# A two-layer graph network on one core: the first chunks of the query and key weights, the value weights and the last weight each in a slot of their own, and the last batch's softmax sums by folds with its norms in another order

## The chip, the cores and the metric

The kernel runs on one core of a Trainium2 chip. The metric is the device time of one execution in microseconds, as the median of several runs. All times below are microseconds (us) of that device time or of the span of one profiled execution.

## The reference

Two layers over a batch of 32 graphs with the same 512 nodes and the same adjacency matrix; each node has 512 features. Everything is float32.

```
x: (32, 512, 512), adj: (512, 512) of zeros and ones, symmetric, ones on its diagonal

def layernorm(x): (x - mean) / sqrt(var + 1e-5)        # over the last axis, no weights

# layer 0: attention over neighbours, 8 heads of 64
q, k, v = x @ Wq + bq, x @ Wk + bk, x @ Wv + bv        # (32, 512, 512), seen as 8 heads of 64
scores  = q k^T / sqrt(64) + (-1e9 where adj == 0)     # (32, 8, 512, 512)
x = layernorm(x + softmax(scores) @ v)

# layer 1: graph convolution
x = layernorm(x + ((adj @ x) @ W1 + b1))
```

## The kernel before

**Units of matmul work.** TensorE (PE) works in 128 by 128 tiles with 512 columns. The products with weights are split products: each float32 operand is split into a high part and a rest of fp32r type, and a product takes three passes, HIGH, REST and BOTH (a combination of the two), of four 128x512 matmuls each. One such unit of 12 matmuls makes 128 columns of q or k (`project`, L396 by way of `one_pass`), 128 rows of v (`project_values`), or 128 rows of the convolution (`convolve`). The parts of an operand are made by three instructions: ACT makes the high part (`split_high` L298, for weights `split_weight` L308), DVE the rest (L301, L309), and POOL or DVE the combination (L304, L312, L318).

**A batch.** For each batch: 8 units for q and k, 4 for v, the scores of four pairs of heads (`scores` L565, 16 matmuls of 64x512 per pair, two pairs at a time in `take_scores`), the mask added by DVE (L567, 16 operations for two pairs) and the exponential by ACT (L569), the sums of the exponentials over the four key blocks by POOL (L580), and the product with v (`attend` L588). Then the aggregation adj times x (`aggregate` L509, for the last batch `aggregate_rows` L530), whose halves are made by `split` (L483, L485) or `split_rows` (L518, L519), and the convolution with its residual (L542, L543). Layer norms are `statistics` (L455, L456), `square_root` (L459 on ACT), `invert_root` (L464, L465 on DVE) and `normalise` (L470 on ACT).

**Order.** The order of all instructions is written by hand: under `manual_schedule` each engine, and SP which issues nearly all DMAs, takes its instructions in the order in which the program calls them, and waits for the data of each. `first_half(b)` runs the product with v for two pairs, the 8 projection units of batch b+1 with other work behind each (the lists in `behind`, merged in by `merge`), and the scores of the other two pairs. `second_half(b)` runs the rest of b's attention, the v units of b+1, b-1's aggregation and convolution, and the first scores of b+1. The last batch has an order of its own, `last_halves`, and a tail in the kernel's main part. `ahead`, `seen` and `next_` there are lists of normalisations and statistics that are put between the units of the last convolutions.

**Slots.** Tiles are named by tags, and a tag has a fixed number of slots. A new tile waits until all readers of the tile that lay in its slot are done. The tags that matter here: `wv` and `w1` (one slot each: the split value weights and the split last weight W1), `xs` (two: adjacency at the start, then batches of x and the raw W1), `stream` (three: chunks of the split q and k weights), `e` (8: raw weights at the start, then exponentials) and `turn` (6: blocks of x).

**Chunks of the query and key weights.** The weights of q and k are split once, in 8 chunks (n = 0 to 7: q0, k0, q1, k1 and so on) by `make_chunk` (ACT and DVE) and `finish_chunk` (DVE), while batch 0 is projected with them. Each is written to DRAM by `keep_chunk` (L383), and from batch 1 on fetched back for each batch by `fetch_chunk` (L391), three ahead; `project` fetches chunk n+3 when it has used chunk n. In the kernel before, chunks 0 to 3 are made in the slot of `wv` and chunks 4 to 7 in that of `w1`:

```
        if n % DB == 0:
            EARLY[n // DB] = work.tile([P, DB, 3, DB, P], FR, name="early", tag=("wv", "w1")[n // DB], bufs=1)
```

So the value weights are split (`split_values_weight`) when chunks 0 to 3 have been written out, and W1 is split (`split_last_weight`) late, at the end of `second_half(0)`; its raw form is loaded before the attention of batch 0.

**Sums of the softmax.** For the sums over the keys, POOL's result still has to be added over 128 partitions and brought to the layout of the rows. In all batches but the last, `fold_squares` does it on DVE: it transposes in squares of 32 (L619) and reduces (L622, twice per pair), and after two pairs writes the parts to DRAM (L627); `fetch_parts` reads them back in four DMAs (L634) and `add_up` adds and inverts (L640, L641). The outputs of these batches come back to rows by way of DRAM too (`turn_out` L602 and L604, `fetch_rows` L610) and are scaled by ACT (L654). The last batch has its sums from PE: `sum_queries` (L670) multiplies by a column of ones, 32 matmuls of one column per two pairs, and `invert_sums` (L676, L677) inverts them. Its outputs are transposed by PE (`turn_back` L685) and scaled and added by DVE (`last_residual` L689, L691).

**Other names.** `stay_warm` issues matmuls on zeros at the start, `load_squares` loads a block of x of a later batch in four DMAs (L232), `look_for_low_half` tests adj, and `judge` makes a verdict on the data, which the 1x1 matmul in the last loop gathers; another kernel for general inputs runs behind it, and does not run for these data.

Of the kernel before, what the change touches and what calls it, by code (L numbers as in the profile page):

```python
# [18 lines left out]
P = 128  # L19
# [163 lines left out]
def fast_kernel(ctx: ExitStack, tc, verdict, x, adj, Wq, bq, Wk, bk, Wv, bv, W1, b1, out):  # L183
# [34 lines left out]

    def load_block(b, c):
        IN[b, c] = work.tile([P, D], FP, name="xin", tag="turn", bufs=TURNS)  # L220
        nc.sync.dma_start(IN[b, c], x[b, c * P:(c + 1) * P, :])

    def load_squares(b, d):

# [135 lines left out]
    SEQUENCE = [(which, m) for m in range(DB) for which in "qk"]  # L360
    CHUNK, KEPT = {}, {}
    AHEAD = 3
    EARLY, MADE = {}, {}

    def chunk():
        return work.tile([P, 3, DB, P], FR, name="stream", bufs=AHEAD)
# [1 line left out]
    def make_chunk(n):  # L368

        which, m = SEQUENCE[n]  # L370
        if n % DB == 0:
            EARLY[n // DB] = work.tile([P, DB, 3, DB, P], FR, name="early", tag=("wv", "w1")[n // DB], bufs=1)
        made = MADE[n] = CHUNK[0, which, m] = EARLY[n // DB][:, n % DB, :, :, :]
        split_weight(made[:, HIGH, :, :], made[:, REST, :, :], RAW[which, m // 2][:, m % 2, :, :])

    def finish_chunk(n):
# [235 lines left out]
    def fold_squares(b, hp):  # L612

        if hp % PAIRS == 0:
            PART[b, hp // PAIRS] = work.tile([P, P // SQ, NB, GROUP], FP, name="part", bufs=1)
        part = PART[b, hp // PAIRS]
        es = ES.pop((b, hp))
        square = SQUARES.pop((b, hp))
        nc.vector.transpose(square.rearrange("p s n -> p (s n)"), es.rearrange("p s n -> p (s n)"))  # L619
        squares = [square[:, s, :] for s in range(2)]  # L620
        for s in range(2):
            nc.vector.tensor_reduce(part[:, :, :, 2 * (hp % PAIRS) + s].rearrange("p i c -> p c i"),  # L622
                                    squares[s].rearrange("p (c i f) -> p c i f", c=NB, f=SQ), axis=AX.X,
                                    op=ALU.add)
        if hp % PAIRS == PAIRS - 1:
            PASSED[b, hp // PAIRS] = passing.tile([P, P // SQ, NB * GROUP], FP, name="passed")
            nc.sync.dma_start(PASSED[b, hp // PAIRS], part.rearrange("p i c h -> p i (c h)"))  # L627
# [29 lines left out]
        cols = X[b][:, :, hp * P:(hp + 1) * P]  # L657
        nc.gpsimd.tensor_add(cols, cols, ROWS.pop((b, hp)))

    SUMS = {}  # L660

    def sum_queries(b, g):

        sums = SUMS[b, g] = bank(NB, GROUP)
        for hp in range(g * PAIRS, (g + 1) * PAIRS):
            es = ES.pop((b, hp))
            for s in range(2):
                for c in range(NB):
                    h = 2 * (hp % PAIRS) + s
                    nc.tensor.matmul(sums[:, c, h:h + 1], es[:, s, c * P:(c + 1) * P], ones[:, 0:1],  # L670
                                     start=True, stop=True)

    def invert_sums(b, g):
        both = work.tile([P, 2, NB, GROUP], FP, name="inverse")
        total, inverse = both[:, 0, :, :], both[:, 1, :, :]
        nc.vector.tensor_copy(total, SUMS.pop((b, g)))  # L676
        nc.vector.reciprocal(inverse, total)  # L677
        nc.gpsimd.tensor_add(watched, watched, both)
        INVERSE[b, g] = inverse

    def turn_back(b, hp):

        pt = OUT[b, hp] = bank(NB, 2, HD)
# [27 lines left out]
    def stay_warm(times):  # L711
        for _ in range(times):
            nc.tensor.matmul(pm, still, still, start=True, stop=True)

    stay_warm(7)
    x_transpose(0)
    x_both(0, nc.gpsimd)
    make_chunk(0)
    stay_warm(4)
    for c in range(1, NB):  # L720
        x_transpose(c)
        x_both(c, nc.gpsimd if c < NB - 1 else nc.vector)
# [2 lines left out]
    make_chunk(1)  # L725
    finish_chunk(0)
    finish_chunk(1)
    for n in range(2):
        keep_chunk(n)

    def split_values_weight(d):
        w = RAW["v", d // 2][:, d % 2, :]
# [1 line left out]
        both_of_weight_beside(wv[:, BOTH, d, :], wv[:, REST, d, :], w)  # L734

    def split_last_weight(d):
        split_weight(w1[:, HIGH, d, :], w1[:, REST, d, :], w1_raw[:, d, :])
        both_of_weight(w1[:, BOTH, d, :], w1[:, HIGH, d, :], w1[:, REST, d, :])

    def norm(t, which):  # L740
# [31 lines left out]
    def first_half(b):  # L772

        attend(b, 0)
        turn_out(b, 0)
        attend(b, 1)
        turn_out(b, 1)
        fold_squares(b, 0)
        seen, old = survey(b - 2)[NB // 2:], norm(b - 1, 1)
        fresh, young = survey(b - 1, 0), norm(b - 1, 0)  # L780
        scaled, added = residuals(b, 0)
        squares = [(load_squares, b + 2, d) for d in range(DB // 2)]
        if b == 0:
            seen = [(look_for_low_half, c) for c in range(NB)]
        behind = [[(fetch_rows, b, 0)] + seen, [(fetch_rows, b, 1), (fold_squares, b, 1)] + old[:1], old[1:4],
                  [(fetch_parts, b, 0)] + old[4:],
                  [(take_scores, b, 1)] + ([(store, b - 2)] if b > 1 else []),
                  [(add_up, b, 0)] + fresh[:2], fresh[2:] + [(load, b)] + scaled[:1], young[:2] + scaled[1:],
                  added + young[2:] + squares]
        units = projections(b + 1)  # L790
        run(merge(units[:4] + [(list,)] + units[4:], behind))

    def second_half(b):

        splits, gathered = aggregation(b - 1)
        scaled, added = residuals(b, 1)
        turned, divided = turns(b + 2), splits_of_x(b + 2)
        squares = [(load_squares, b + 2, d) for d in range(DB // 2, DB)]
        early_seen = survey(b - 1) if b < B - 2 else []
        attend(b, 2)  # L800
        turn_out(b, 2)
        run(squares[:1])
        fold_squares(b, 2)
        attend(b, 3)
        fetch_rows(b, 2)
        turn_out(b, 3)
        fold_squares(b, 3)
        run(squares[1:])
        fetch_rows(b, 3)
        fetch_parts(b, 1)  # L810
        units = values(b + 1)
        if b == 0:
            run(units[:2] + [(take_scores, 1, 0)] + units[2:] + turned + divided + [(add_up, 0, 1)] + scaled + added)
            run([(split_last_weight, d) for d in range(DB)])
            return
        run(merge(units, [splits[:1], splits[1:2], splits[2:3], splits[3:] + turned[:1]]) + biases(b - 1))
        run(merge(gathered, [turned[1:2], turned[2:3], turned[3:] + [(add_up, b, 1)]]))
        if b == B - 2:
            load(B - 1)
        take_scores(b + 1, 0)  # L820
        run(merge(convolution(b - 1)[:NB if b < B - 2 else NB // 2],
                  [scaled[:1], early_seen[:1], early_seen[1:2]]))
        run(divided + scaled[1:] + added)

    def last_halves(b):

        splits, gathered = aggregation(b - 1)
        attend(b, 0)
        turn_out(b, 0)
        attend(b, 1)  # L830
        turn_out(b, 1)
        sum_queries(b, 0)
        take_scores(b, 1)
        turn_back(b, 0)
        turn_back(b, 1)
        run(survey(b - 1, 0) + norm(b - 1, 0))
        run(convolution(b - 2)[NB // 2:] + [(invert_sums, b, 0)] + splits)
        attend(b, 2)
        turn_out(b, 2)
        attend(b, 3)  # L840
        turn_out(b, 3)
        run([(last_residual, b, 0), (last_residual, b, 1)])
        turn_back(b, 2)
        turn_back(b, 3)
        sum_queries(b, 1)
        run(gathered[:2] + [(invert_sums, b, 1), (last_residual, b, 2), (last_residual, b, 3)] + gathered[2:])

    units = projections(0)
    ends = project_first_two()
# [2 lines left out]
        finish_chunk(n)  # L852
    run(ends)
    adjacency(0)
    for n in range(2, 4):
        keep_chunk(n)
    for d in range(2):
        load_squares(1, d)
    wv = None
    for n in range(2, len(units)):  # L860
        if n + 2 < len(units):
            make_chunk(n + 2)
# [1 line left out]
        run(units[n:n + 1])  # L864
        if n < 5:
            adjacency(n - 1)
        elif n == 5:
            wv = work.tile([P, 3, DB, N], FR, name="wv", bufs=1)
        if n > 4:
            split_values_weight(n - 5)  # L870
    split_values_weight(DB - 1)
    for n in range(4, len(units)):
        keep_chunk(n)
    for n in range(AHEAD):
        fetch_chunk(len(SEQUENCE) + n)
    for d in range(2, DB):
        load_squares(1, d)
    w1 = work.tile([P, 3, DB, N], FR, name="w1", bufs=1)
    w1_raw = work.tile([P, DB, D], FP, name="xs", bufs=2)
    nc.sync.dma_start(w1_raw, W1.rearrange("(c p) f -> p c f", p=P))  # L880
    b1_r = load_row(nc, consts, b1, "b1_r")
    take_scores(0, 0)
    run(merge(values(0), [[unit] for unit in turns(1)]))
# [8 lines left out]
    rest, final = convolution(t - 1), convolution(t)  # L892
    ahead, seen, next_ = norm(t, 0), survey(t - 1), norm(t, 1)
    run(biases(t - 1) + survey(t, 0) + ahead[:2])
    run(rest[:1])
    for c in range(NB):
        run(ahead[2 + c:3 + c])
        split_rows(t, c)
        run(rest[1 + c:2 + c])
    for c in range(NB):  # L900
        add_bias(t, c)
    run(survey(t - 2) + norm(t - 1, 1))
    store(t - 2)
    run(seen + next_[:2])
    aggregate_rows(t)
    well = judge()
    for table, name, shape in ((STAT, "stat", (2 * NB, 2)), (RSTD, "rstd", (2 * NB,)), (SHIFT, "shift", (2 * NB,))):
        table[t + 1] = work.tile([P, *shape], FP, name=name, bufs=3)
    for r, unit in enumerate(final):
# [9 lines left out]
        else:  # L919
            normalise(t + 1, NB + r)  # L920
        store(t, [r])
        if r == 0:
            run(next_[2:])
            store(t - 1)
        if r == 1:
            pm = bank(N)
            nc.tensor.matmul(pm[0:1, 0:1], well, ones[:, 0:1], start=True, stop=True)
# [25 lines left out]
```

## Time and profile before

| | us |
|---|---|
| three runs | 2655.01, 2658.06, 2660.86 |
| their median | 2658.06 |
| the profiled execution | 2655.91 |
| its span | 2654.1 |
| PE busy | 2621.1 (99%) |
| DVE busy | 2178.0 (82%) |
| POOL busy | 1765.3 (67%) |
| ACT busy | 1592.3 (60%) |

The mean granted TensorE clock of the profiled execution is 0.993 of full speed. Shares of busy time are shares of the span. In the views that follow, an engine's idle time is listed before the instruction that it waited for, with an arrow to what released it; where several semaphores were waited for, the one named is that which came last by the profile. "PEld" is TensorE's weight load, "SPq" the queue of SP, which issues DMAs.

### The profile page before, as it was taken

The page shows a single profiled execution, that of the slowest core. Times are in us where ns is not written, and L with a number is a line of the kernel's source. Part 1 is how long each engine was busy: PE and PEld are TensorE (multiplying, and loading weights), DVE is VectorE, ACT ScalarE, POOL GpSimd, SP SyncE. Part 2 cuts the span into 40 slices and gives each one's busy share as a digit, 9 for nine tenths or more (in the row PEclk, how much of TensorE's full clock was granted, in tenths as well). Part 3 has the DMA queues.
Part 4 walks back from the last instruction along what each step waited for, and adds up shares of the span by engine and source line. Part 5 has one row for each costly group of instructions (what it writes and reads, how often), then busy time and mean ns, then how long its engine had stood idle before and what let it go on. Part 6 is the DMA issues. An engine that isn't in the chain of part 4 may idle for free.

```text
span 2654.1 us, 35600 instructions
## 1 busy us (share of the span) xinstructions
PE 2621.1 (99%) x11394; PEld 1717.2 (65%) x11394; DVE 2178.0 (82%) x3513; ACT 1592.3 (60%) x2618; POOL 1765.3 (67%) x1087
## 2 busy tenths in 40 slices
PE   9989999999999999999999999999999999999997
PEld 6556666666666666666666666666666666666665
DVE  7868888888888888888888888888888888888867
ACT  4457556566556575565665565765665755656653
POOL 4556677676686666776766766666766667667663
PEclk9989999999999999999999999999999999999999
DMA  8565445664446654456644456544466544565411
GB/s 250 161 161 152 110 119 150 177 170 136 115 119 169 177 159 113 120 139 177 174 148 111 116 159 177 160 125 116 130 177 176 149 110 121 152 177 163 122 33 49
DMA packets 672832, 379.28 MB, mean 143 GB/s; under 512 B 585344, under 2 KB 589440, under 8 KB 672640
## 3 DMA queue, kind: packets, MB, share of 16 engines
q1 hardware_dynamic: 672640, 376.95, 51.8%
q8 instruction: 92, 1.51, 0.2%
q14 instruction: 100, 0.82, 0.1%
HBM read 302.45 MB, written 74.38 MB: 142 GB/s over the span
## 4 chain that ended last, share of the span: by engine, by line
PE 94%; DMA 2%; DVE 2%; ACT 1%; SPq 1%; issue 0%; DVEq 0%; ACTq 0%
PE bank L396 50%; PE bank L565 18%; PE bank L588 17%; PE bank L509 9%; DMA stream<-kept_k 2%; DVE factors L301 0%; DVE bnst L455 0%; DMA xin<-in_x_dram 0%; PE bank L670 0%; SPq L240 0%; ACT rows L654 0%; SPq L232 0%; DMA xs<-in_adj_dram 0%; DVE w L309 0%; DVE wv L309 0%
## 5 line engine op out<-in xcount | busy, mean ns | idle before, releaser
L396 PE MATMUL bank<-factors,stream 128*128 128x512 f32 x2976 | 703.1, 395 | 12.7 <-DMA stream<-kept_k 10.3
L396 PEld LDWEIGHTS bank<-factors,stream 128*128 128x128 f32 x2976 | 555.5, 189 | 182.5 <-issue 41.8
L580 POOL TENSOR_TENSOR es<-e 128x1024 f32<-128x1024 f32 x128 | 306.8, 2397 | 527.6 <-ACT e L569 527.6
L567 DVE SCALAR_TENSOR_TENSOR e<-gap,bank 128x512 f32<-128x512 uint8 x1024 | 617.3, 678 | 15.0 <-PE bank L565 14.8
L580 POOL TENSOR_TENSOR es<-es,e 128x1024 f32<-128x1024 f32 x256 | 614.2, 2399 | 20.1
L569 ACT ACTIVATE e<-e 128x1024 f32<-128x1024 f32 x512 | 509.8, 1050 | 47.7 <-DVE e L567 31.6
L304 POOL TENSOR_TENSOR factors<-factors,factors 128x512 fp32r<-128x512 f32 x253 | 359.1, 1434 | 213.0 <-DVE factors L301 212.1
L565 PE MATMUL bank<-q,k 64*128 64x512 f32 x2048 | 480.7, 604 | 2.6 <-ACT q L407 1.9
L588 PE MATMUL bank<-e,v 128*64 128x512 f32 x2048 | 453.6, 595 | 0.0
L565 PEld LDWEIGHTS bank<-q,k 64*128 64x128 f32 x2048 | 219.6, 187 | 233.6 <-issue 153.8
L396 PE MATMUL bank<-w,factors 128*128 128x512 f32 x1536 | 361.7, 394 | 4.2 <-ACT factors L298 3.3
L654 ACT ACTIVATE rows<-rows,zero,inverse 128x64 f32<-128x64 f32 x992 | 341.0, 426 | 31.1 <-POOL es L580 22.2
L298 ACT ACTIVATE factors<-bank 128x512 fp32r<-128x512 f32 x132 | 78.5, 597 | 468.4 <-PE bank L509 464.0
L396 PE MATMUL bank<-wv,factors 128*128 128x512 f32 x1536 | 357.8, 392 | 0.0
L396 PEld LDWEIGHTS bank<-w,factors 128*128 128x128 f32 x1536 | 286.3, 188 | 88.7 <-ACT e L569 22.7
L396 PEld LDWEIGHTS bank<-wv,factors 128*128 128x128 f32 x1536 | 285.7, 188 | 84.8 <-ACT xs L470 24.3
L588 PEld LDWEIGHTS bank<-e,v 128*64 128x64 f32 x2048 | 141.4, 137 | 278.4 <-issue 276.3
L509 PE MATMUL bank<-adjT,halves 128*128 128x512 f32 x960 | 229.6, 396 | 0.0
L470 ACT ACTIVATE xs<-xs,shift,rstd 128x512 f32<-128x512 f32 x248 | 184.1, 803 | 48.7 <-DVE shift L465 48.7
L509 PEld LDWEIGHTS bank<-adjT,halves 128*128 128x128 f32 x960 | 180.8, 188 | 43.6
L407 ACT ACTIVATE q<-bank,bq_c 128x512 f32<-128x512 f32 x128 | 86.9, 679 | 194.9 <-PE bank L396 194.9
L487 POOL TENSOR_TENSOR halves<-xs,halves 128x512 fp32r<-128x512 f32 x120 | 151.8, 1298 | 62.3 <-ACT halves L483 62.3
(96 smaller groups left out, 2522.1 us busy)
## 6 DMA issues: line engine op xcount, KB each, us to landing
stream<-kept_q SPq DMA_DIRECT2D x124, 768.0 KB, 6.1
stream<-kept_k SPq DMA_DIRECT2D x124, 768.0 KB, 5.0
xin<-in_x_dram SPq DMA_DIRECT2D x496, 64.0 KB, 2.8
turned<-attT SPq DMA_DIRECT2D x124, 256.0 KB, 2.3
rows<-turned SPq DMA_DIRECT2D x496, 64.0 KB, 3.6
xs<-in_x_dram SPq DMA_DIRECT2D x31, 1024.0 KB, 7.1
out_dram<-xs SPq DMA_DIRECT2D x31, 1024.0 KB, 5.5
part<-passed SPq DMA_DIRECT2D x248, 8.0 KB, 3.6
```

The lines of the kernel that those rows point to most:

```text
L304: engine.tensor_sub(both, plain(high), plain(rest))
L396: nc.tensor.matmul(pm, left(f, d), right(f, d), start=(f != REST and d == 0), stop=(f != HIGH and d == DB - 1))
L407: nc.scalar.activation(t, near, AF.Identity, bias=bias[:, m:m + 1], scale=1.0 + EPSILON)
L470: nc.scalar.activation(row, row, AF.Identity, bias=SHIFT[t][:, slot:slot + 1], scale=RSTD[t][:, slot:slot + 1])
L487: nc.gpsimd.tensor_sub(low, cols, plain(high))
L509: nc.tensor.matmul(pm, part, adjT[:, n % NB, :], start=(n == 0), stop=(n == 2 * NB - 1))
L565: nc.tensor.matmul(ps[s], keys[:, j * P:(j + 1) * P], queries, start=True, stop=True)
L567: nc.vector.scalar_tensor_tensor(e[:, s, :], gap[:, j, :], NEG * root, ps[s], op0=ALU.mult, op1=ALU.add)
L569: nc.scalar.activation(e, e, AF.Exp, scale=1.0 / root)
L580: nc.gpsimd.tensor_add(ES[b, hp], ES[b, hp] if j > 1 else E[b, hp, 0], E[b, hp, j])
L588: nc.tensor.matmul(po[s * HD:(s + 1) * HD, :], V[b, j][:, h * HD:(h + 1) * HD], e[:, s, :], start=(j == 0), stop=(j == NB - 1))
L654: nc.scalar.activation(part, part, AF.Identity, bias=zero, scale=inverse[:, c, s:s + 1])
```

## The change

- Of batch 0's four blocks of x, the second and fourth are loaded from ACT's queue; two of the matmuls of `stay_warm` go.
- Chunks 0 to 3 lie in one tile in the slot of `w1`, chunks 4 to 6 in the three slots of `stream`, and chunk 7 in one slot of `xs`. `wv` has its slot from the start. `split_values_weight` stands behind units 4 to 7 instead of 5 to 7 and their end. The writes of all chunks stand after the units, chunks 0 to 2, then half the squares of x of batch 1, chunks 3 to 7, the other squares, and the first three fetches.
- W1 is loaded in `first_half(0)`, behind the third unit, and split behind the first unit of `first_half(1)`.
- The last batch has its sums by `fold_squares`, `fetch_parts` and `add_up` like the others; `sum_queries` and `invert_sums` go. The order of the statistics, norms and biases of the last three batches changes, and `store` of the last but one batch stands before the last convolution.

```
     def load_block(b, c):
-        nc.sync.dma_start(IN[b, c], x[b, c * P:(c + 1) * P, :])
+        (nc.scalar if c % 2 else nc.sync).dma_start(IN[b, c], x[b, c * P:(c + 1) * P, :])
...
     def make_chunk(n):
-        if n % DB == 0:
-            EARLY[n // DB] = work.tile([P, DB, 3, DB, P], FR, name="early", tag=("wv", "w1")[n // DB], bufs=1)
-        made = MADE[n] = CHUNK[0, which, m] = EARLY[n // DB][:, n % DB, :, :, :]
+        if n < DB:
+            made = early[:, n, :, :, :]
+        elif n < DB + AHEAD:
+            made = chunk()
+        else:
+            made = work.tile([P, 3, DB, P], FR, name="last_chunk", tag="xs", bufs=2)
+        MADE[n] = CHUNK[0, which, m] = made
...
     def fold_squares(b, hp):
-        square = SQUARES.pop((b, hp))
-        nc.vector.transpose(square.rearrange("p s n -> p (s n)"), es.rearrange("p s n -> p (s n)"))
-        squares = [square[:, s, :] for s in range(2)]
+        if b == B - 1:
+            squares = [work.tile([P, N], FP, name="square", tag="turn", bufs=TURNS) for _ in range(2)]
+            for s in range(2):
+                nc.vector.transpose(squares[s], es[:, s, :])
+        else:
...
-    def sum_queries(b, g):
...
-    def invert_sums(b, g):
...
+    early = work.tile([P, DB, 3, DB, P], FR, name="early", tag="w1", bufs=1)
     stay_warm(7)
...
-    stay_warm(4)
+    stay_warm(2)
...
-    for n in range(2):
-        keep_chunk(n)
+    def load_last_weight():
+        RAW["w1"] = work.tile([P, DB, D], FP, name="xs", bufs=2)
+        nc.sync.dma_start(RAW["w1"], W1.rearrange("(c p) f -> p c f", p=P))
...
     def first_half(b):
         if b == 0:
-            seen = [(look_for_low_half, c) for c in range(NB)]
+            seen, old = [(look_for_low_half, c) for c in range(NB)], [(list,), (load_last_weight,)]
+        if b == 1:
+            seen = [(split_last_weight, d) for d in range(DB)]
...
     def second_half(b):
         if b == 0:
             run(units[:2] + [(take_scores, 1, 0)] + units[2:] + turned + divided + [(add_up, 0, 1)] + scaled + added)
-            run([(split_last_weight, d) for d in range(DB)])
             return
...
     def last_halves(b):
         attend(b, 0)
         turn_out(b, 0)
+        fold_squares(b, 0)
         attend(b, 1)
         turn_out(b, 1)
-        sum_queries(b, 0)
         take_scores(b, 1)
         turn_back(b, 0)
         turn_back(b, 1)
-        run(survey(b - 1, 0) + norm(b - 1, 0))
-        run(convolution(b - 2)[NB // 2:] + [(invert_sums, b, 0)] + splits)
+        fold_squares(b, 1)
+        fetch_parts(b, 0)
+        run(survey(b - 1, 0) + norm(b - 1, 0) + convolution(b - 2)[NB // 2:] + splits)
         attend(b, 2)
         turn_out(b, 2)
         attend(b, 3)
         turn_out(b, 3)
-        run([(last_residual, b, 0), (last_residual, b, 1)])
         turn_back(b, 2)
         turn_back(b, 3)
-        sum_queries(b, 1)
-        run(gathered[:2] + [(invert_sums, b, 1), (last_residual, b, 2), (last_residual, b, 3)] + gathered[2:])
+        run([(add_up, b, 0)] + folds(b, 1) + [(fetch_parts, b, 1), (last_residual, b, 0), (last_residual, b, 1)])
+        run(merge(gathered, [[unit] for unit in survey(b - 2)]) + norm(b - 1, 1))
+        store(b - 2)
+        run([(add_up, b, 1), (last_residual, b, 2), (last_residual, b, 3)])
...
-    for n in range(2, 4):
-        keep_chunk(n)
-    for d in range(2):
-        load_squares(1, d)
-    wv = None
+    wv = work.tile([P, 3, DB, N], FR, name="wv", bufs=1)
     for n in range(2, len(units)):
...
-        elif n == 5:
-            wv = work.tile([P, 3, DB, N], FR, name="wv", bufs=1)
-        if n > 4:
-            split_values_weight(n - 5)
-    split_values_weight(DB - 1)
-    for n in range(4, len(units)):
+        if n > 3:
+            split_values_weight(n - 4)
+    for n in range(AHEAD):
         keep_chunk(n)
+    for d in range(2):
+        load_squares(1, d)
+    for n in range(AHEAD, len(units)):
+        keep_chunk(n)
+    for d in range(2, DB):
+        load_squares(1, d)
     for n in range(AHEAD):
         fetch_chunk(len(SEQUENCE) + n)
-    for d in range(2, DB):
-        load_squares(1, d)
     w1 = work.tile([P, 3, DB, N], FR, name="w1", bufs=1)
-    w1_raw = work.tile([P, DB, D], FP, name="xs", bufs=2)
-    nc.sync.dma_start(w1_raw, W1.rearrange("(c p) f -> p c f", p=P))
...
     run(biases(t - 1) + survey(t, 0) + ahead[:2])
-    run(rest[:1])
     for c in range(NB):
         run(ahead[2 + c:3 + c])
         split_rows(t, c)
-        run(rest[1 + c:2 + c])
+        run(rest[c:c + 1] + seen[c:c + 1])
     for c in range(NB):
         add_bias(t, c)
-    run(survey(t - 2) + norm(t - 1, 1))
-    store(t - 2)
-    run(seen + next_[:2])
+    run(next_[:2])
     aggregate_rows(t)
+    run(next_[2:])
+    store(t - 1)
     well = judge()
...
-        if r == 0:
-            run(next_[2:])
-            store(t - 1)
```

More of the change, by code (lines that the diff above doesn't have):

```diff
@@ L362, in fast_kernel @@
     AHEAD = 3
-    EARLY, MADE = {}, {}
+    MADE = {}
     def chunk():
@@ L617, in fold_squares @@
         es = ES.pop((b, hp))
-        square = SQUARES.pop((b, hp))
-        nc.vector.transpose(square.rearrange("p s n -> p (s n)"), es.rearrange("p s n -> p (s n)"))
-        squares = [square[:, s, :] for s in range(2)]
+        if b == B - 1:
[3 more added lines that the diff above has]
+        else:
+            square = SQUARES.pop((b, hp))
+            nc.vector.transpose(square.rearrange("p s n -> p (s n)"), es.rearrange("p s n -> p (s n)"))
+            squares = [square[:, s, :] for s in range(2)]
         for s in range(2):
@@ L658, in add_rows @@
         nc.gpsimd.tensor_add(cols, cols, ROWS.pop((b, hp)))
-    SUMS = {}
-    def sum_queries(b, g):
[L664 to L671, printed above, removed]
-    def invert_sums(b, g):
[L674 to L679, printed above, removed]
     def turn_back(b, hp):
@@ L736, in split_last_weight @@
     def split_last_weight(d):
-        split_weight(w1[:, HIGH, d, :], w1[:, REST, d, :], w1_raw[:, d, :])
+        split_weight(w1[:, HIGH, d, :], w1[:, REST, d, :], RAW["w1"][:, d, :])
         both_of_weight(w1[:, BOTH, d, :], w1[:, HIGH, d, :], w1[:, REST, d, :])
```

## The prediction

> **What bounds the kernel now.** I read the page first: its busy times and the chain that ended last.
>
> ```profile
> PE 2621.1 (99%) x11394; PEld 1717.2 (65%) x11394; DVE 2178.0 (82%) x3513; ACT 1592.3 (60%) x2618; POOL 1765.3 (67%) x1087
> PE 94%; DMA 2%; DVE 2%; ACT 1%; SPq 1%; issue 0%; DVEq 0%; ACTq 0%
> ```
>
> TensorE (PE) works 2621.1 of 2654.1 us; only the 33 us in which it doesn't can be won without taking matmuls away. The view by windows says where they lie (columns: window, length, busy time of PE, its weight loads, DVE, ACT, POOL, then granted clock, DMA share, GB/s):
>
> ```profile
> 20.00:40.00 20.00, 16.57 (x66) 11.36 (x65) 13.31 (x22) 9.07 (x17) 1.63 (x2) 0.95 0.94 294
> 130.00:160.00 30.00, 19.27 (x57) 12.65 (x57) 19.09 (x27) 10.02 (x24) 8.00 (x7) 0.72 0.45 117
> 200.00:300.00 100.00, 100.00 (x437) 66.07 (x436) 84.92 (x140) 63.49 (x104) 70.24 (x43) 1.00 0.43 117
> 2560.00:2580.00 20.00, 20.00 (x96) 11.11 (x93) 7.31 (x13) 8.98 (x15) 11.54 (x7) 0.83 0.00 0
> 2620.00:2640.00 20.00, 16.64 (x62) 11.74 (x61) 17.80 (x44) 7.35 (x14) 5.54 (x4) 0.91 0.14 52
> 2640.00:2655.00 15.00, 4.53 (x20) 3.38 (x19) 6.53 (x18) 4.46 (x8) 0.00 (x0) 0.81 0.39 144
> ```
>
> Idle PE: 3.4 us in 20:40, 10.7 in 130:160, 3.4 and 10.5 at the end, none in 200:300. The order of the instructions of the two programs agrees on every engine, waits included, from the middle of the second batch to the last; so whatever is won at 40 or 160 us is carried to the end by a PE that is never idle, and only three stretches need a sum. I read each in the timeline (start, duration, engine, line; idle time before and its releaser in brackets):
>
> ```profile
> 29.79 0.63 ACT L283 ACTIVATE adjT<-attT 128x512 fp32r<-128x512 f32 x1 [2.13 <-DVE attT L282]
> 36.11 0.63 ACT L308 ACTIVATE wv<-e 128x512 fp32r<-128x512 f32 x1 [4.59 <-DMA xin<-in_x_dram]
> 42.00 9.64 DVE L567 SCALAR_TENSOR_TENSOR e<-gap,bank 128x512 f32<-128x512 uint8 x16
> ...
> 139.37 1.35 DVE L309 SCALAR_TENSOR_TENSOR w<-xs,w 128x512 fp32r<-128x512 f32 x1 [6.05 <-ACT w L308]
> 147.12 0.41 SPq L391 DMA_DIRECT2D stream<-kept_k  x1
> 152.06 5.46 PE L396 MATMUL bank<-factors,stream 128*128 128x512 f32 x12 [8.38 <-DMA stream<-kept_k]
> 158.67 9.65 DVE L567 SCALAR_TENSOR_TENSOR e<-gap,bank 128x512 f32<-128x512 uint8 x16 [0.35 <-PE bank L565]
> ...
> 2565.18 4.98 PE L670 MATMUL bank<-ones,es 128*128 128x1 f32 x32
> 2570.09 9.33 PE L565 MATMUL bank<-q,k 64*128 64x512 f32 x32
> 2572.26 1.28 DVE L567 SCALAR_TENSOR_TENSOR e<-gap,bank 128x512 f32<-128x512 uint8 x2 [13.30 <-PE bank L565]
> 2594.12 3.63 PE L670 MATMUL bank<-ones,es 128*128 128x1 f32 x32
> 2629.55 0.30 ACT L459 ACTIVATE rstd<-stat,eps 128x4 f32<-128x4 f32 x1 [0.27 <-DVE stat L456]
> 2642.27 0.17 DVE L464 RECIPROCAL rstd<-rstd 128x1 f32<-128x1 f32 x1 [1.54 <-ACT rstd L459]
> ```
>
> At 36.11 ACT waits 4.59 us for wv's slot. Chunks 0 to 3 lie there, and the last of their writes to DRAM, issued at 24.67, lands 11.3 us later (the longest of L383), at 36.0; the DMA named only landed last. At 139.37 DVE, which has W1 to split, has stood 6.05 us; the fetch at 147.12 is queued behind what DVE does after that, and PE stands 8.38 us for it. At 2572.26 DVE stands 13.30 us, the last 5 behind 32 matmuls of sums. Line numbers here are those of before.
>
> **Start: minus 4.3.** With wv in a slot of its own the 4.59 us wait goes. DVE then starts wv's first split at 30.97, 0.76 after ACT began at 30.32 as in the other splits, and has nine operations of 0.69 before the masks: four wv splits, two for chunk 7, three evictions (units 5 to 7). 30.97 + 9 x 0.69 = 37.2; 0.5 more because wv's splits took 1.03 and 1.00 beside POOL instead of 0.69: 37.7. ACT's work (36.3) is done earlier. The masks began at 42.00, so 4.3; all splits at 0.69 give 4.8, all slow with a wait between 3. What is late next is PE, filled by these scores and then the values, whose weights POOL finishes in time.
>
> SP: all eight writes, sixteen squares of x and three fetches, 27 issues, now stand from 23.2 on in one row. They move 6.3 + 1.0 + 2.4 MB; at the 418 GB/s that 42:44 shows that is 23 us, so the fetches land near 48 to 57. PE wants the first at 66.09 - 4.3 = 61.8: hidden. Were every issue as slow as the eight squares of before (11.76 / 8 = 1.47 each) and landing 9.6, as the first fetches: 23.2 + 27 x 1.47 + 9.6 = 72.5, a stall of 10.7.
>
> Two of x's first blocks go through ACT's queue, and two warming matmuls go. Bytes and engines of the transfer are the same, SP issues less by two (0.4 to 0.5 each), ACT more by two: taken as 0, from -0.5 to +0.7. The Trainium skill speaks against a gain here: "DMA: Bandwidth & Descriptors", Rules for kernel authors, says that spreading issues over engines brings no bandwidth, only issue time; no run here separates the two yet.
>
> **Middle: minus 8.3.** W1's split (per block one ACT and two DVE operations; eight DVE operations, 139.37 to 145.4) stands ahead of the transposes (L602, two, 1.30), the turned writes, the fetch at 147.12 and the folds. Now it stands behind the first projection unit of the next batch. From the end of the row L641 (133.33) the transposes end at 134.65, and the fetch is issued when unit 0 gives its slot back, near 136. With 4.8 to land (147.12 to 151.9) it is there at 141; PE ends units 0 to 2 at 143.67 and so has nothing to wait for. DVE: a fold to 137.1, a wait for ACT's 16 rows (to 138.8) and its eviction of q, an eviction to 140.1, the four splits at 1.33 and 0.65 for POOL's contention to 145.9, an eviction, a fold of 2.5, two evictions: 150.4. The masks began at 158.67: 8.3. If PE's clock or POOL took 2 us back, 6; if DVE's wait were shorter, 9. Later fetches: the next is issued near 149.5 and lands by 156, needed at 159.2. Hidden.
>
> Loading W1 (1 MB, 1.60 to issue, 6.3 to land) moves ahead of the fetch for which PE has until 90.95; that was issued at 79.22, now 2 later, and fetches took 4.8 to 9.6. Hidden; uncovered it would cost up to the 1.6 us.
>
> **End: minus 5.5.** The 64 one-column matmuls (4.98 + 3.63) go. Scores of pair 1 start at 2565.2 instead of 2570.09, and masks 1.25 later at full clock (2.17 at the 0.83 of this window): 2566.45, which is 5.8 earlier. In exchange DVE gets four folds of 2.5 (two transposes, two reductions, as at 146.59 to 149.1). The first is free, within the 13.30 us. From 2566.45 DVE is the chain: masks 9.64, fold 2.5, statistics 4 x 0.82, root 0.66, four evictions 2.78, low halves 3.41, sums' inversion 0.5, two folds 5.0, two residuals 2.74, four splits with statistics 4 x (0.66 + 0.82), root 0.66, inversion 0.5, two residuals 2.74, statistics 3.28, root 0.8. The sum is 44.4; with 0.25 of small waits 2611.1, where the row L470 has 2613.39: only 2.3 remain of 5.8. Four blocks of 2.8 (split, two evictions, statistics) from 2612.95 end at 2624.1, and the square root comes at 2624.3 instead of 2629.55: 5.2, since the older batch's statistics no longer follow here. In the final rounds L464 waits 1.54 once behind four normalisations on ACT (the other rounds 0.36); they move ahead, another 1.2. Ideal 6.4; with PE's last aggregation, which DVE now gates until 2623.9, 4.9. I take 5.5, between 2.5 (folds unhidden and parts late) and 6.5.
>
> The sums go through DRAM: SP issues one write and four reads per group (1.6 + 2.1), and these reads land 3.6 after issue in the median: group 0 at 2585.8, wanted at 2588.9; group 1 at 2602, wanted at 2603.8. A margin of 2 to 3. The stores of the two older batches (1 MB each) move ahead on SP, but stand behind the second reads and before the last rows' stores, whose rows are not ready until later: 0.
>
> A second rule is weighed at PE's gaps in this stretch. By the rows: PE stood 1.92 us before 37.88, and the granted clock was then 0.53 in 38:40 and 0.61 in 40:42, 1.00 in 42:44. So a gap of 2 us takes about 2 us of clock. The Trainium skill, "TensorE: Matmul & The Clock Gate", Part 1, lets the clock fall only after an idle window of about 3.4 us; by it such gaps would cost nothing beyond themselves, and the sum would be 6.4 at the end.
>
> **Sum.** 4.3 + 8.3 + 5.5 = 18.1: span 2636.0, profiled execution 2655.91 - 18.1 = 2637.8. The median of the runs lies 2.15 above the profiled one, so 2658.06 - 18.1 = 2640.0. A measurement of this kernel can tell about 0.2% (5.3 us) from no change.
>
> **Rivals.**
> Folds eat the end: DVE is the chain there and 10 us of folds take back what 8.6 us of matmuls gave. For: only 2.3 of 5.8 survive at 2611. Against: the reordered statistics and roots. 2658.06 - 12.6 = 2645.5. Chance 0.18.
> Fetches late: SP's 27 issues at 1.47, stall 10.7, start at +6.4 instead of -4.3: 2650.7; half of it 2645. For: the squares' pace at 25.61. Against: the bytes. 0.10.
> Slower, the clock: in the last batch PE waits for DVE in many small gaps, and the clock stays near half from 2586 on. Some 160 matmuls at 0.232 more are 37 us, less 4 already lost and 12 covered by PE's idle time: +21 against -18.1, 2661. It decides only if over nine tenths of them run at half; the clock was back within 4 us at 42. 0.07.
> It doesn't do what it says: the gain of the middle is taken back where the second batch waits for something unseen (a slot, x's squares), leaving 4 or less of the sum: 2654 to 2658. 0.05.
>
> **How the numbers follow.** The forecast has 0.60: 2635 to 2645 from the bounds of its terms (11.5 to 20) and 2 us of spread between runs. The range 2632 to 2650 adds the first rival and most of the second. Faster by over 0.2% is 0.60 + 0.18 + 0.10 = 0.88, within 0.05, slower 0.07.
>
> **What would show it.** Right: the first masks at 37 to 38; no 4.59 before wv; PE idle in 130:160 down from 10.7 to about 3, with no wait for the fetch; the masks at 150; no L670; the four-column square root near 2624 less the earlier 12.6; no 1.54 in the final rounds. Wrong: PE waiting for the stream near 62; DVE idle before the parts' reduction in the last batch; a clock under 0.8 there; or idle PE between 200 and 2540.

## The result

The changed kernel takes 2638.05 us (four runs, 2636.07 to 2638.50), the kernel before 2656.53 on the same chip (2654.63 to 2660.86): ratio 0.9927, 95% interval 0.9914 to 0.9939, or 18.5 us less, where 18.1 was forecast. Run again on another chip it took 2637.19 against 2654.64 (0.9934, 0.9921 to 0.9948), 17.5 less. The profiled execution is 2636.07 us with a span of 2634.3, the quickest of its four.

The page of the changed kernel, its busy times and the chain that ended last (line numbers from here on are those of each kernel; the changed one has L571 for the masks, L395 for the fetch, L463 for the root):

```profile
PE 2607.4 (99%) x11326; PEld 1706.5 (65%) x11326; DVE 2186.5 (83%) x3529; ACT 1592.2 (60%) x2618; POOL 1765.0 (67%) x1087
PE 93%; DVE 3%; DMA 1%; issue 1%; POOL 1%; ACT 1%; SPq 0%; DVEq 0%; POOLq 0%; ACTq 0%
```

PE's idle time fell only from 33.0 to 26.9 us, but its busy time fell by 13.7 as well: 68 records fewer (64 of the matmuls with ones and 4 of the two warming matmuls, which the trace shows as two records each), and less time at a low clock. DVE has 8.5 us more work. The same by windows (columns as before):

```profile
20.00:40.00 20.00, 16.97 (x66) 11.49 (x66) 17.18 (x25) 10.60 (x19) 4.78 (x4) 0.91 0.96 323
130.00:160.00 30.00, 28.14 (x106) 18.72 (x106) 25.52 (x43) 20.45 (x37) 14.47 (x10) 0.94 0.62 173
2560.00:2580.00 20.00, 17.83 (x81) 11.03 (x80) 18.29 (x37) 11.90 (x16) 12.13 (x6) 0.91 0.03 5
2580.00:2600.00 20.00, 17.61 (x73) 13.07 (x71) 16.99 (x38) 8.11 (x14) 10.39 (x9) 1.00 0.16 56
2600.00:2620.00 20.00, 17.20 (x60) 11.44 (x61) 18.13 (x39) 8.77 (x16) 8.11 (x6) 0.91 0.14 53
```

In 130:160 PE now works 28.1 of 30 us, with 106 matmuls where there were 57. From 2560 on it is idle about 2 to 3 us in every 20, spread thin, beside a DVE that is busy 17 to 18: the last batch is DVE's. The timeline at the places that the prediction named:

```profile
29.20 0.63 ACT L283 ACTIVATE adjT<-attT 128x512 fp32r<-128x512 f32 x1 [2.13 <-DVE attT L282]
31.42 1.65 DVE L309 SCALAR_TENSOR_TENSOR last_chunk<-e,last_chunk 128x512 fp32r<-128x512 f32 x1 [0.35 <-ACT last_chunk L308]
35.51 1.46 DVE L309 SCALAR_TENSOR_TENSOR wv<-e,wv 128x512 fp32r<-128x512 f32 x1
37.50 1.43 DVE L309 SCALAR_TENSOR_TENSOR wv<-e,wv 128x512 fp32r<-128x512 f32 x1
38.85 9.64 DVE L571 SCALAR_TENSOR_TENSOR e<-gap,bank 128x512 f32<-128x512 uint8 x16
...
132.99 0.32 SPq L395 DMA_DIRECT2D stream<-kept_k  x1
146.50 9.64 DVE L571 SCALAR_TENSOR_TENSOR e<-gap,bank 128x512 f32<-128x512 uint8 x16
...
2553.82 9.65 DVE L571 SCALAR_TENSOR_TENSOR e<-gap,bank 128x512 f32<-128x512 uint8 x16 [5.07 <-PE bank L569]
2573.51 2.50 DVE L489 TENSOR_TENSOR low<-xs,high 128x512 fp32r<-128x512 f32 x4 [0.93 <-ACT high L487]
2611.07 0.30 ACT L463 ACTIVATE rstd<-stat,eps 128x4 f32<-128x4 f32 x1 [7.63 <-DVE stat L460]
2622.51 0.17 DVE L468 RECIPROCAL rstd<-rstd 128x1 f32<-128x1 f32 x1 [0.36 <-ACT rstd L463]
```

The 4.59 us wait ahead of wv is gone, and the masks start without one; the fetch that PE stood 8.38 us for is issued at 132.99 instead of 147.12; DVE's 13.30 us wait is 5.07; the last rounds show 0.36 where one showed 1.54.

**By stretches.** Since PE is full between, the gain is read between fixed points: from ACT's first adjacency copy to the first masks (start), from these to the masks at 146.50 (middle), from there to the masks at 2533.94, and from those to the end of the span (end).

| | before | changed | difference | forecast |
|---|---|---|---|---|
| up to the first adjacency copy | 18.23 | 17.64 | -0.59 | 0 |
| start | 23.77 | 21.21 | -2.56 | -4.3 |
| middle | 116.67 | 107.65 | -9.02 | -8.3 |
| 2387 us between | 2387.85 | 2387.44 | -0.41 | 0 |
| end | 107.58 | 100.36 | -7.22 | -5.5 |
| span | 2654.1 | 2634.3 | -19.8 | -18.1 |

The first and the fourth row are scatter: with the same code the first copy came between 17.64 and 18.18, and the part between took from 2387.2 to 2391.1 in the runs below.

### The profile page after: what moved, and what is told of

It reads as the page before. It is cut to its first block, busy times and chain, and to the rows that moved or that the text cites. A ratio compares the mean times of both kernels' runs of the same rounds, so it can differ in the third digit from the quotient of the medians.

```text
span 2634.3 us, 35500 instructions
## 1 busy us (share of the span) xinstructions
PE 2607.4 (99%) x11326; PEld 1706.5 (65%) x11326; DVE 2186.5 (83%) x3529; ACT 1592.2 (60%) x2618; POOL 1765.0 (67%) x1087
## 4 chain that ended last, share of the span: by engine, by line
PE 93%; DVE 3%; DMA 1%; issue 1%; POOL 1%; ACT 1%; SPq 0%; DVEq 0%; POOLq 0%; ACTq 0%
PE bank L400 51%; PE bank L569 17%; PE bank L592 16%; PE bank L513 9%; DMA stream<-kept_k 1%; DVE bnst L459 0%; DVE e L571 0%; POOL es L584 0%; DVE factors L301 0%; PE bank L534 0%; POOL factors L304 0%; DVE part L631 0%; SPq L240 0%; DMA xs<-in_adj_dram 0%; DVE square L625 0%
## 5 line engine op out<-in xcount | busy, mean ns | idle before, releaser
L584 POOL TENSOR_TENSOR es<-e 128x1024 f32<-128x1024 f32 x128 | 306.8, 2397 | 512.6 <-ACT e L573 512.6
L584 POOL TENSOR_TENSOR es<-es,e 128x1024 f32<-128x1024 f32 x256 | 614.2, 2399 | 20.1
L571 DVE SCALAR_TENSOR_TENSOR e<-gap,bank 128x512 f32<-128x512 uint8 x1024 | 617.3, 678 | 6.0 <-PE bank L569 5.9
```

The lines of the kernel that those rows point to most:

```text
L571: nc.vector.scalar_tensor_tensor(e[:, s, :], gap[:, j, :], NEG * root, ps[s], op0=ALU.mult, op1=ALU.add)
L584: nc.gpsimd.tensor_add(ES[b, hp], ES[b, hp] if j > 1 else E[b, hp, 0], E[b, hp, j])
```

## Experiments

Each run is read in two ways: its median against the kernel before on the same chip, and its profile by the same stretches, which scatter by some 0.3 us.

| kernel | median | before, same chip | difference | start | middle | end |
|---|---|---|---|---|---|---|
| changed | 2638.05 | 2656.53 | -18.5 | 21.21 | 107.65 | 100.36 |
| s1_old_start | 2638.68 | 2654.28 | -15.6 | 22.63 | 107.88 | 100.61 |
| s2_split_late | 2645.31 | 2654.28 | -9.0 | 21.20 | 116.46 | 100.67 |
| s3_old_end | 2644.34 | 2654.28 | -9.9 | 21.21 | 107.66 | 108.09 |
| s4_x_sp | 2637.04 | 2654.28 | -17.2 | 21.22 | 107.68 | 100.61 |
| s5_ones_sums | 2643.68 | 2656.40 | -12.7 | 21.24 | 107.69 | 106.58 |
| s6_old_norms | 2638.51 | 2656.40 | -17.9 | 21.20 | 107.68 | 100.98 |
| s7_pool_later | 2638.20 | 2656.40 | -18.2 | 21.22 | 107.72 | 100.36 |
| s8_copies_later | 2634.00 | 2656.40 | -22.4 | 17.41 | 107.74 | 100.39 |
| s9_pool_turned | 2635.19 | 2654.64 | -19.5 | 18.81 | 108.28 | 100.53 |
| s10_both | 2631.06 | 2654.64 | -23.6 | 15.01 | 108.30 | 100.48 |
| s11_after_again | 2637.19 | 2654.64 | -17.5 | 21.20 | 107.65 | 100.62 |

### One part taken back at a time

**s1_old_start**: chunks 0 to 3 in the slot of `wv`, 4 to 7 in that of `w1`, and the writes where they stood before.

```
-        if n < DB:
-            made = early[:, n, :, :, :]
...
+        if n % DB == 0:
+            EARLY[n // DB] = work.tile([P, DB, 3, DB, P], FR, name="early", tag=("wv", "w1")[n // DB], bufs=1)
+        made = MADE[n] = CHUNK[0, which, m] = EARLY[n // DB][:, n % DB, :, :, :]
```

> The changed kernel with the slots and the writes of the chunks as before (value weights behind chunks 0 to 3 again, x's blocks and W1 as changed). Theory that each of the three stretches gives its own share and PE carries it to the end: masks of batch 0 begin near 41.4 instead of 38.85, and the span is 2.6 us longer than the changed kernel's (the 0.6 of x's blocks stays). Rival, that the slots only move work and the gain is x's blocks: no change.

Only the start changes, by 1.42 instead of 2.6. ACT's wait for wv's slot is back, but shorter than before the change:

```profile
34.47 0.63 ACT L308 ACTIVATE wv<-e 128x512 fp32r<-128x512 f32 x1 [3.44 <-DMA xin<-in_x_dram]
```

The last of the four writes is issued at 23.69 here, at 24.67 before, and it landed after 10.6 instead of 11.3 us. Counted from the first adjacency copy, which itself came 0.5 sooner here, the issue is 0.5 earlier. So this start is 1.1 us shorter than that of the kernel before, and what differs in it are x's blocks on ACT's queue and the two warming matmuls. That SP, with two blocks of x less to issue, came to the write earlier is the likely reason for the 0.5. It is not shown, because no run has the old slots with all of x from SP, and why the write landed 0.7 quicker stays open. Once wv has its own slot, x's blocks are worth nothing (s4).

**s2_split_late**: W1's load and split where they stood before.

```
-            seen = [(split_last_weight, d) for d in range(DB)]
...
+            run([(split_last_weight, d) for d in range(DB)])
```

> The changed kernel with W1 loaded before the first attention and split at the end of the first second half, as before. Theory: the wait for the fetch (about 8.4 us) and the late folds are back, the masks of the next pairs begin 9 us later, and the span is 9 us longer than the changed kernel's. Rival, that the slots of the start already made room: less than 3 us.

Middle 8.81 us longer, as the theory has it, and the wait is back in the timeline. Part of its price is the clock: the 12 matmuls behind it take 5.46 us, where 48 take 11.17 at 152.47 in the changed kernel.

```profile
149.25 5.46 PE L400 MATMUL bank<-factors,stream 128*128 128x512 f32 x12 [8.23 <-DMA stream<-kept_k]
155.84 9.65 DVE L571 SCALAR_TENSOR_TENSOR e<-gap,bank 128x512 f32<-128x512 uint8 x16 [0.34 <-PE bank L569]
```

**s3_old_end**: `last_halves` and the tail of the kernel before, whole.

```
+        sum_queries(b, 0)
...
-    run(next_[2:])
-    store(t - 1)
...
+        if r == 0:
+            run(next_[2:])
+            store(t - 1)
```

> The changed kernel with the last batch and the tail as before (sums by ones on PE, norms and stores in the old order). Theory: the span is 7.2 us longer than the changed kernel's, all of it behind 2540. Rival, that folds eat what the sums on PE gave: 0 to 2 us. Forecast's term: 5.5.

End 7.73 us longer (7.2 expected), the other stretches equal. Taken back one by one, start, middle and end cost 1.4, 8.8 and 7.7 us, and each run changes its own stretch alone, so none hides another. That is 18.0 of the 18.8 us that the three stretches gained. The 1.1 us of the start that s1 does not give back belongs to x's blocks or the warming matmuls, as said there.

**s4_x_sp**: all blocks of x from SP.

```
-        (nc.scalar if c % 2 else nc.sync).dma_start(IN[b, c], x[b, c * P:(c + 1) * P, :])
+        nc.sync.dma_start(IN[b, c], x[b, c * P:(c + 1) * P, :])
```

> The changed kernel with all blocks of x of batch 0 issued by SP again. Theory A, that the earlier issue brought the 0.6 us by which the first stage (adjacency transposed, 29.79 before, 29.20 after) came earlier: 0.6 us later there, and the same at the end. Theory B, the note that spreading issues brings nothing: 0, the 0.6 then comes from the two warming matmuls or from the order of DVE.

The first copy came at 17.57, 0.07 earlier than the changed kernel's. Theory A is refuted. The 0.6 is also not the warming matmuls': s2, which lacks the two like the changed kernel, had its first copy at 18.18, and the unedited changed kernel (s11) had it at 18.12. So the 0.6 lies inside the scatter of the first loads.

### What in the end brings the gain

**s5_ones_sums**: the sums by matmuls with ones, the changed order of norms.

```
+        sum_queries(b, 0)
         take_scores(b, 1)
...
-        run([(add_up, b, 0)] + folds(b, 1) + [(fetch_parts, b, 1), (last_residual, b, 0), (last_residual, b, 1)])
+        sum_queries(b, 1)
+        run([(invert_sums, b, 0), (last_residual, b, 0), (last_residual, b, 1)])
```

**s6_old_norms**: the folds, but statistics, norms and stores of the last three batches in the old order.

```
-        run(merge(gathered, [[unit] for unit in survey(b - 2)]) + norm(b - 1, 1))
-        store(b - 2)
+        run(gathered)
...
+    run(survey(t - 2) + norm(t - 1, 1))
+    store(t - 2)
+    run(seen + next_[:2])
```

> The changed kernel, but the last batch has its sums from 64 one-column matmuls on PE as before, in the changed order of norms. Theory A, that the end's gain is the matmuls that went: masks of the last pairs 5.8 us later, end 5 to 6 us later. Theory B, that on DVE's chain the folds take back what the matmuls gave, and the gain is the order of norms: masks 5.8 later, then three folds of 2.5 less on DVE, so the last batch's first norm comes 1.7 earlier and the end is 0 to 2 us earlier than the changed kernel's.

> The changed kernel with its folds, but statistics, norms, biases and stores of the last three batches in the old order. Theory A (matmuls): end 0 to 2 us later, the 1.2 for the wait behind ACT's normalisations. Theory B (order): 5 to 7 us later than the changed kernel, with PE idle before the last convolution again, as in the kernel before (3.31 us there).

At the end theory A holds in both: with ones 6.2 us longer, with the old norms only 0.6. The last masks of s5 missed what was expected: they came 3.9 us later than in the changed kernel, not 5.8 (23.74 us behind the masks before them, against 19.88). The first 32 matmuls with ones took 3.73 us here and 4.98 in the kernel before. The timeline of s5 shows where the matmuls sit on the path:

```profile
2573.33 2.10 DVE L469 SCALAR_TENSOR_TENSOR shift<-stat,rstd 128x4 f32<-128x4 f32 x1
...
2582.20 3.63 PE L679 MATMUL bank<-ones,es 128*128 128x1 f32 x32
2585.69 2.01 PE L513 MATMUL bank<-adjT,low 128*128 128x512 f32 x4
2587.50 1.85 PE L513 MATMUL bank<-adjT,high 128*128 128x512 f32 x4
...
2590.03 0.69 DVE L301 SCALAR_TENSOR_TENSOR factors<-factors,bank 128x512 fp32r<-128x512 f32 x1 [5.21 <-ACT factors L298]
```

The aggregation waits behind the 3.63 us of ones, and DVE, which has no folds to do, stands 5.21 us for it. In the changed kernel DVE folds in that time. The first eight matmuls of the aggregation take 3.9 us instead of the 2.2 of the later ones (the clock granted in 2580:2590 is 0.83), but they take 3.4 in the changed kernel too (2.06 + 1.36, behind a gap of 2.17), so the clock at this place is little of what the ones cost. It counts behind the first group of ones: the 32 matmuls of the scores take 8.9 us there, 9.33 in the kernel before and 7.28 in the changed kernel.

Not all of the 6.2 us need be the ones'. The small operation L469, which takes 0.16 us in the changed kernel at the same step, takes 2.10 here, and it ends with an addition of POOL's (L584, 2573.06 to 2575.42). That can be up to 1.9 us of the path, so the ones are worth 4.3 to 6.2 us (an estimate from these rows). s3 has the same wait (1.90 us), and its end is 0.5 longer than that of the kernel before. Theory B, an end 0 to 2 us earlier, is out either way.

s6 gives back 1.2 us in the final rounds (19.1 us from the four-column root to the last normalisation, 17.9 in the changed kernel) and has that root 0.8 sooner, counted from the masks.

### Why the start came out small

**s7_pool_later**: POOL's four subtractions (L318) collected and issued behind the loop.

```
-        nc.gpsimd.tensor_sub(both, plain(rest), plain(temp))
+        LATER.append((nc.gpsimd.tensor_sub, both, plain(rest), plain(temp)))
...
+    run(LATER)
```

> The changed kernel with POOL's four subtractions for the value weights issued behind the last chunk's split instead of beside each. The term of the start was 4.3 and came out at 2.6, from the fourth adjacency copy to the masks. Theory, that DVE's splits were slowed beside POOL (1.65, 1.46 and 1.43 us instead of 0.69): they take 0.69 again and the masks begin 1.7 to 2.5 us earlier, 7.2 to 8 after that copy instead of 9.65. Rival, that ACT or PE paces this stretch: 9.65 stays, and DVE has waits instead.

Nothing changed, and nothing could: POOL has no other work there, so its own order stayed the same and each subtraction still ran as soon as its split was made. The run is a repeat of the changed kernel.

**s9_pool_turned**: the same list, in reverse.

```
-    run(LATER)
+    run(LATER[::-1])
```

> The changed kernel with POOL's four subtractions for the value weights in the reverse order, so that the first of them waits for the last split and all stand behind DVE's splits (the mere shift of the last trial left POOL's own order as it was, so it changed nothing). Theory, that DVE is slowed beside POOL: the splits take 0.69 instead of 1.65, 1.46 and 1.43, and the masks begin 2.5 us earlier, about 7.2 after the fourth adjacency copy instead of 9.65. Rival, that ACT or PE paces it: 9.65 with waits on DVE.

```profile
31.88 0.69 DVE L309 SCALAR_TENSOR_TENSOR last_chunk<-e,last_chunk 128x512 fp32r<-128x512 f32 x1 [0.35 <-ACT last_chunk L308]
35.01 0.68 DVE L309 SCALAR_TENSOR_TENSOR wv<-e,wv 128x512 fp32r<-128x512 f32 x1
36.89 9.64 DVE L573 SCALAR_TENSOR_TENSOR e<-gap,bank 128x512 f32<-128x512 uint8 x16
37.12 4.97 POOL L695 TENSOR_TENSOR wv<-wv,temp 128x512 fp32r<-128x512 f32 x4 [25.30 <-DVE wv L309]
```

The splits that took 1.65, 1.46 and 1.43 take 0.69, and the masks begin 7.24 after the fourth copy: 2.4 us earlier, as the theory has it. 0.6 of it is lost again in the middle, where x's four splits (L301) now meet POOL's sums of the exponentials and take 5.91 us instead of 4.61.

**s8_copies_later**: ACT's adjacency copy behind the next chunk's first split.

```
-        nc.scalar.activation(adjT[:, c, :], turned, AF.Copy)
+        COPIES.append((nc.scalar.activation, adjT[:, c, :], turned, AF.Copy))
...
             finish_chunk(n + 2)
+        run(COPIES)
+        COPIES.clear()
```

> The changed kernel with ACT's copy of each adjacency block put behind the next chunk's first split instead of ahead of it. Before each chunk DVE stands 0.76 us for that split, four times. Theory, that DVE paces the start: the masks begin 2.3 to 3.0 us earlier and so does the end. Rival, that PE's projection units or the weights' loads pace it: under 1 us.

From first copy to masks it is 3.8 us less, more than the 3.0 expected. DVE's four waits of 0.76 go, and with them one of 0.35 ahead of chunk 7's split. The remaining 0.4 is overlap: DVE's operations start some 0.09 us before the end of the one before (18.10 against 18.19), and one that has to wait does not. So the time from one adjacency copy to the next falls by 0.85 and not 0.76 (from 3.85 to 3.00).

**s10_both**: s8 and s9 together.

> Reversed subtractions and the later adjacency copies together. The copies alone brought the masks 3.7 us earlier. Theory: the gains add, since DVE paces both stretches: masks near 33, end 5.5 to 6.5 us before the changed kernel's. Rival, that PE's last units or the fetches for the next batch (they were issued at 47.8 in any case) take over: no more than the 4 us of the copies alone.

The start is 6.2 us shorter than the changed kernel's, the 3.8 of s8 and the 2.4 of s9, and the run 6.1 (2631.06, 2630.61 to 2632.43, against 2637.19, 2636.54 to 2638.14, on the same chip). Against the kernel before the ratio is 0.9911 (0.9895 to 0.9926). This version beats both kernels.

**s11_after_again**: the changed kernel, unedited.

> The changed kernel itself, on the same chip as the two others: span between 2634 and 2638, the masks 9.65 us behind the fourth adjacency copy, 17 to 19 us below the kernel before.

It behaved as expected (2635.4 us of span, start 21.20).

## Why the prediction was right, and where it was not

**Bound and method: right.** Only three stretches moved; the 2387 us between gave 0.4, inside its scatter.

**Start: the mechanism right, the size wrong.** The term "0.5 more because wv's splits took 1.03 and 1.00 beside POOL" was the step that failed. Three of DVE's nine operations took 1.65, 1.46 and 1.43, 2.5 us above 3 x 0.69, and s9 puts 2.4 of it down to POOL. So the term was 2.0 too small where 1.7 is missing (2.56 against 4.3). A wait of 0.35 ahead of chunk 7's split was left out as well, and some 0.5 came back because DVE's operations, shown as 0.69 long, start 0.60 apart. The prediction's own "all splits at 0.69 give 4.8" fits s9, whose start is 4.96 shorter than before. A slip of reading changed nothing: 30.97 is 0.65 behind 30.32, and the 0.76 is how long DVE stood.

**SP's row of 27 issues: hidden, as forecast.** The first fetch went out at 47.17 and was wanted at 62.95, and no fetch up to 160 us took more than 8.3. The rival's 10.7 us stall did not come; one later fetch cost 0.63 at 72.03.

**x's blocks and warming: 0, as taken.** For x's blocks s4 shows it; no run puts the two warming matmuls back. Not foreseen was the 1.1 us by which the start with the old slots is shorter than before (s1), and its cause is open between the two.

**Middle: right, 0.7 too small.** The four splits took 5.4 us (136.90 to 142.32), without the 0.65 added for POOL. (The terms put the end of the splits at 140.1 + 4 x 1.33 + 0.65 = 146.1 where the prediction has 145.9; 150.4 comes out all the same.) The wait for the fetch was the cause, as s2 shows.

**End: the sum near, its explanation wrong.** Masks came 5.8 us earlier, as worked out. DVE's chain up to the last batch's norm ran 0.8 quicker than the sum, the low halves in 2.50 instead of 3.41 among it (before, an addition of POOL's ran beside them until 2591.08). The ideal 6.4 was right, and the caution that took 5.5 (PE gated by DVE) was not needed: 6.4 + 0.8 is the 7.2 measured. But the text gave the order of statistics as the reason why 2.3 grows to 5.2. s6 has the old order and loses 0.6: counted from the masks, its last batch's norm begins 2.9 us sooner, because DVE has fewer statistics ahead of it, and from there to the four-column root it takes 2.1 longer. So moved statistics cost DVE nearly the same wherever they stand. What shortened the path is that PE's matmuls with ones went, 4.3 to 6.2 us by s5, with the slow clock behind the first group of them. The rival "folds eat the end" fell for the same reason: without folds DVE only waits.

**The clock: a small matter.** In the changed kernel it went to 0.50 behind gaps near 2 us, for some 3 to 4 us, and came back; no stretch of the last batch stayed low. In s10 PE's clock was 1.00 in 2600:2606 and its last aggregation ended 1 us before it was wanted, with the same end (100.48), where the changed kernel had 0.50 in 2604:2606. So a slow clock at that place cost the end nothing, and it does not decide between the two sums, 5.5 and 6.4, that the prediction weighed.

## What to carry to other kernels

Where one engine is full for almost the whole run, forecast only the stretches where it isn't, and measure between fixed points in the timeline, because the full part scatters by more than a small edit is worth. An operation moved to a loaded engine can still pay if that engine otherwise waits for the one that is relieved: ask what each would wait for without it. And moving an instruction in the program changes nothing on an engine that has nothing else to do; to delay it, give it something to wait for.

## What the runs showed of the hardware

DVE beside POOL. In the repeat of the changed kernel POOL's subtraction (L318) and DVE's split (L309), both of which read two operands in SBUF, show this:

```profile
31.71 1.29 POOL L318 TENSOR_TENSOR wv<-wv,temp 128x512 fp32r<-128x512 f32 x1 [19.85 <-DVE wv L309]
31.91 1.63 DVE L309 SCALAR_TENSOR_TENSOR last_chunk<-e,last_chunk 128x512 fp32r<-128x512 f32 x1 [0.35 <-ACT last_chunk L308]
```

DVE's split ends 0.54 after POOL's end at 33.00, so DVE did not run slower, it waited for nearly all of POOL's instruction. In the changed kernel the two other long splits end 0.54 behind POOL's as well (36.97 against 36.43, 38.93 against 38.39). Operations with one operand in PSUM kept their time (the masks 0.60 each, the evictions 0.68). The Trainium skill, "SBUF — State Buffer", Who interferes with whom, fits this: it says that a DVE instruction with two SBUF inputs contends with a GpSimd (POOL) instruction that reads SBUF, and that the ports which the two share are an exclusive lock. A split costs what is left of POOL's instruction, not a percentage.

The clock behind a gap. In the changed kernel PE stood 1.87 us before 31.44, and the windows show (granted clock is the figure behind POOL's):

```profile
32.00:34.00 2.00, 1.52 (x5) 0.97 (x4) 1.97 (x3) 2.00 (x5) 0.52 (x1) 0.75 0.95 144
34.00:36.00 2.00, 2.00 (x6) 1.52 (x6) 2.00 (x4) 1.38 (x4) 0.86 (x1) 0.50 0.90 253
```

In its repeat, with a gap of 1.84 at the same place, the clock is 1.00 in both. So a gap of about 2 us sometimes halves the clock and sometimes doesn't. The clock also fell without a gap: in the kernel before, PE was busy for all of 2565:2574, at first with the 32 one-column matmuls with ones, and the granted clock was 0.74 in 2565:2570 and 0.50 in 2570:2574. The Trainium skill, "TensorE: Matmul & The Clock Gate", Part 1, has a window that runs free of the program, which agrees with that chance; that it takes an idle window of about 3.4 us does not agree with a drop behind 1.87, nor with one behind no gap.
